# Queries and keys of an attention layer, stored in the order of the products and fetched 128 rows at a time

## The chip, the core and the metric

The kernel runs on one NeuronCore of a Trainium2 chip. A core has five engines that work side by side, each with its own queue, which it works off in order: TensorE (PE) multiplies matrices and writes into PSUM; VectorE (DVE) reduces and combines; ScalarE (ACT) applies functions such as exp; GpSimd (POOL) does the rest; SyncE (SP) issues transfers. Transfers (DMAs) between memory (DRAM) and the core's SBUF are carried out by 16 DMA engines; SP, ACT and POOL can issue them, and an issuing engine that has to wait before it issues holds up everything behind it in its queue.

The metric is the device time of one execution in microseconds (us). Of the kernel before, three runs gave 1357.38, 1358.45 and 1362.58 us; the median is 1358.45 us.

## The reference, cut to what matters

One decoder layer on x of 4 x 1024 tokens x 256 features: self-attention with 16 heads of 16 features, cross-attention to 64 context tokens, and a feed-forward part with ternary weights, each after a layer norm and added to x. The change touches the self-attention only:

```python
qkv = x @ W_qkv + b_qkv                      # x: (B, N, 256), layer-normed
q, k, v = jnp.split(qkv, 3, axis=2)          # each to (B, N, 16 heads, 16)
energy = jnp.einsum('bqhe,bkhe->bqhk', q, k)
attn = jax.nn.softmax(energy, axis=-1) / sqrt(E)
out = jnp.einsum('bihv,bvhd->bihd', attn, v)
x = x + out.reshape(B, N, E) @ W_out + b_out
```

## The kernel before

**Split numbers.** A query or key is kept as two parts: a rounded high part (float32r) and the low rest. One product over 64 rows gives all four cross terms of a head: its rows hold the query as high, high, low, low (16 rows each) and the key as high, low, high, low. A tile `q` or `k` (128 rows x 1024 tokens) holds two heads, 64 rows each: a pair.

**Stages of the self-attention.** The work is cut in 16 units: batch b (4) times group g of four heads (4), and a unit has two pairs. Before a unit come

- `ln1(b)` (L334): layer norm of the batch's x. Statistics on DVE (`bn_stats`, L241), a square root on ACT (L247; its function table has to be loaded, and exp's table again afterwards), normalising (on ACT, L258, after the start-up), transposing on PE, copying out of PSUM on ACT (L279).
- `project(b, c)` (L351): queries and keys of eight heads. For each side (q, k) and each half of the tokens (512), PE makes the product, ACT writes the high part into a tile `hl` (L369), DVE the low part (L370), and one DMA of 512 KB stores `hl` in DRAM (L375) in a tensor of the form part (2) x feature (128) x token (1024). In the very first project, three of the four stores are issued from ACT, and their `hl` come from another set of buffers. Else `hl` has two buffers, and a buffer is free again when its store is done.
- `fetch(u)` (L378): fills the two pairs of `q` and `k` of unit u from those tensors. Each 16 rows of a tile are one DMA of 16 rows x 1024 tokens (64 KB, L393): 32 DMAs for a unit, all on SP. For unit 0 the tokens are taken in halves, so there are 64 DMAs of 32 KB, 16 of them issued from ACT. Buffers of `q` and `k` are four each, so fetch(u + 1) waits until the scores of unit u - 1 are done.

**The order of the work.** PE's, SP's and the pool's DMA order is the program's own order (`ordered`, L54). At the start: `ln1(0)`, `project(0, 0)`, three pieces of it woven into `ln1(0)`; `fetch(0)`; four pieces of `project(0, 1)` (L873); then 16 calls of `top()` (L883), of which every second is followed by a piece of `values(0)`. `top()` is one step of `maxima(u)` (L423): two products of 128 queries with 512 keys and the maximum over the keys on DVE (L446, tile `mx`). The maxima of half a unit are joined (`nm`, L455), rounded (`nm_s`, L458 and L459), transposed on PE and copied out by ACT as `mT` (L464). Then `fetch(1)` is issued, then x of batch 1 (`load_x(1)`, L890), then small weights.

The main loop (L914) has 16 steps for each unit. A step makes the scores of a key block, both pairs (products `q,k` and `mT,sel`, then exp on ACT, L911, tile `exp`), two steps of maxima for the half unit that comes next, and the product of older `exp` tiles with the values. Between them `fill()` puts pieces of `ln1` and `project` of later batches and of the post-processing of earlier ones, by credits that grow towards a due step. `fetch(u + 1)` is called in steps 0 and 1 of unit u; the maxima that need its tiles begin at step 8. After the 16 units the feed-forward part remains.

The order of DVE's and ACT's instructions is not written out: a scheduler places them when the program is built, by the times that it expects, transfers included. Each transfer issued from SP or ACT counts on one of eight semaphores, which are used in turn; a transfer that reuses one waits until the transfer before it on that semaphore has landed. So at most eight are under way.

Of the kernel before, what the change touches and what calls it, by code (L numbers as in the profile page):

```python
# [9 lines left out]
F32 = mybir.dt.float32  # L10
# [7 lines left out]
B, S, E = 4, 1024, 256  # L18
H, D = 16, 16
SK = 64  # L20
HID = 1024
P = 128
# [8 lines left out]
def decoder_layer(ctx, tc, a, out):  # L31
# [15 lines left out]
    nc = tc.nc  # L47
# [14 lines left out]
    def dma(**kwargs):  # L62
        ordered(nc.sync.dma_start(**kwargs))
# [38 lines left out]
    for name in ("wq", "wk"):  # L102
# [5 lines left out]
        t = const.tile([P, E // P, H, D], F32, name=name)  # L108
# [4 lines left out]
    for name in ("bq", "bk"):  # L113

        t = const.tile([P, 2], F32, name=f"{name}_c")
        for g in range(NG):
            r = 64 * (g % 2)
            dma(
                out=t[r : r + 64, g // 2 : g // 2 + 1],
                in_=a[name].rearrange("(j e) g -> g j e", e=32)[g, :, 1 : 1 + D],  # L120
# [35 lines left out]
    dram = main_stack.enter_context(tc.tile_pool(name="dram", bufs=1, space=DRAM))  # L156
# [4 lines left out]
    for i in range(3):  # L161
        t = (const if i else main).tile([P, NT, VW], F32, tag=f"v_sb{i}", name=f"v_sb{i}")
# [28 lines left out]
    def bank():  # L191
        return ps[state["banks"]]()
# [4 lines left out]
    def product(out, terms, start=True, stop=True):  # L197

        n = len(terms)
        strips = [slice(32 * j, 32 * j + 32) for j in range(4)] if state["split"] else [slice(0, P)]  # L200
        for i, (lhsT, rhs) in enumerate(terms):
            for r in strips:
                matmul(
                    out[r, :], lhsT=lhsT[:, r], rhs=rhs, start=start and i == 0,
                    stop=stop and i == n - 1,
                )
# [125 lines left out]
    xnT_of, qk_of, split_of, m_of, pieces_of = {}, {}, {}, {}, {}  # L332

    def ln1(b):  # L334
        mv = main.tile([P, NT, 2], F32, tag="mv1", name="mv1", bufs=2)
        rs = main.tile([P, NT], F32, tag="rs1", name="rs1", bufs=2)
        xnT_of[b] = xnT = main.tile([P, 2, S], F32, tag="xnT", name="xnT")
        n = NT if state["split"] else NT // 2
        for i0 in range(0, NT, n):
            for i in range(i0, i0 + n, 2):  # L340
                yield "free"
                ln_stats(main, mv, [(i + k, b * NT + i + k) for k in range(2)])
            yield "free"
            ln_rstd(main, rs[:, i0 : i0 + n], mv[:, i0 : i0 + n, :])
            for i in range(i0, i0 + n, 4):
                yield "free"
                xn = ln_normalised(post_pool, mv, rs, i, b * NT + i, 4)
                yield "rows"
                ln_transposed(xnT[:, :, i * P : (i + 4) * P], xn)

    def project(b, c):  # L351

        split_of[b, c] = [
            dram.tile([2, P, S], F32, tag=f"kept_{name}", name=f"kept_{name}", bufs=6) for name in "qk"
        ]
        first = (b, c) == (0, 0)

        for side, half in ((0, 0), (1, 0), (1, 1), (0, 1)):
            w, bias = (wq, wk)[side], bqk[("bq", "bk")[side]][:, c : c + 1]
            hl = main.tile([P, 2, 512], F32, tag="exp" if first and half else "hl", name="hl", bufs=4 if first and half else 2)  # L360
            width = 256 if state["split"] else 512
            for i0 in range(0, 512, width):
                yield "cols+"
                cols, part = slice(half * 512 + i0, half * 512 + i0 + width), slice(i0, i0 + width)
                pq = bank()[:, 0:width]
                product(
                    pq, [(w[:, i, c * P : (c + 1) * P], xnT_of[b][:, i, cols]) for i in range(2)]
                )
                nc.scalar.activation(hl[:, 0, part].bitcast(F32R), pq, AF.Identity, bias=bias)  # L369
                nc.vector.scalar_tensor_tensor(  # L370
                    hl[:, 1, part], pq, bias, hl[:, 0, part], ALU.add, ALU.subtract
                )
            cols = slice(half * 512, (half + 1) * 512)
            issue = nc.scalar.dma_start if first and (side or half) else dma
            issue(out=split_of[b, c][side][:, :, cols].rearrange("l p t -> p l t"), in_=hl)  # L375
            pieces_of[b, c] = pieces_of.get((b, c), 0) + 1

    def fetch(u):  # L378

        b, g = divmod(u, NG)  # L380
        pairs = qk_of[u] = []
        rest = []
        for pair in range(2):
            q = main.tile([P, S], F32R, tag="q", name="q", bufs=4)
            k = main.tile([P, S], F32R, tag="k", name="k", bufs=4)
            pairs.append((q, k))
            kept_q, kept_k = split_of[b, g // 2]
            f0 = 64 * (g % 2) + 32 * pair

            def parts(t, kept, order, n, cols, issue, f0=f0):  # L390
                for i, part in enumerate(order):
                    r, f = 64 * n + 16 * i, f0 + 16 * n
                    issue(out=t[r : r + 16, cols].bitcast(F32), in_=kept[part, f : f + 16, cols])  # L393

            if u:
                halves = (slice(0, S),)
            else:
                halves = (slice(0, 512), slice(512, S))
            for n in range(2):
                parts(q, kept_q, (0, 0, 1, 1), n, halves[0], dma)  # L400
            for cols in halves:
                for n in range(2):
                    parts(k, kept_k, (0, 1, 0, 1), n, cols, dma if u or n else nc.scalar.dma_start)
            for n in range(2):
                for cols in halves[1:]:
                    rest.append((parts, q, kept_q, (0, 0, 1, 1), n, cols, dma))
            if pair:
                for f, *args in rest:
                    f(*args)
            yield  # L410

    def values(b):
# [422 lines left out]


    first, parts = ln1(0), project(0, 0)
    for _ in range(10):
        next(first)
# [3 lines left out]
    run(parts)  # L843
    state.update(split=True, pinned=False)
    run(fetch(0))

    sel_f = post_pool.tile([P, 2, P], F32, tag="xn", name="sel_f", bufs=2)
    nc.gpsimd.memset(sel_f, 0.0)
    sel = main.tile([P, 2, P], F32R, name="sel")
    for pair in range(2):  # L850

        for n in range(2):
            c = 64 * n + 2 * pair
# [17 lines left out]


    parts = project(0, 1)  # L873
    for _ in range(5):
        next(parts)
# [11 lines left out]
    run(turning.popleft())  # L887
    due.credit = 0.0
    run(fetch(1))
    load_x(1)  # L890
    loading = late_loads()
# [22 lines left out]
    for u in range(NU):  # L914
        b, g = divmod(u, NG)
# [4 lines left out]
        if g == 0:  # L920
            if b == 0:
                later.add(context(), 6)
                later.add(value_bias(), 1)

            for n in ((1, 2), (), (3,), ())[b]:
                if n > 2:
                    load_x(n)
                due.add(ln1(n), 2)
                due.add(project(n, 0), 8)
                due.add(values(n), 8)  # L930
                if n == 1:
                    due.add(project(n, 1), 8)
            if b % 2:

                due.add(project(b // 2 + 2, 1), 8)
            if b == B - 1:
                load_x(0, view=x_kept, slot=1)
# [4 lines left out]
        for step in range(2 * NT):  # L942
# [3 lines left out]
            if step < 2 and 0 < u < NU - 1:  # L946
                if step == 0:
                    while pieces_of.get(divmod((u + 1) // 2, NG // 2)) != 4:
                        due.step()
                    fetching = fetch(u + 1)  # L950
                next(fetching)
# [151 lines left out]
    halves = 2 * B  # L1103
# [3 lines left out]
    tag = later.tag  # L1107
    while tag is not None or narrows:
        turn += 1
        if tag is not None and turn % 5 in (0, 2):  # L1110
            exps += "Exp" in tag
            tag = next(last, None)
            continue
        sources = []
        if wides:
            i = halves - len(wides)
# [72 lines left out]
```

## Time and profile before

| | before |
|---|---|
| median of three runs | 1358.45 us |
| the profiled execution: its time, its span | 1359.89 us, 1358.1 us |
| PE busy | 1282.7 us (94%), mean granted clock 0.978 |
| DVE busy | 1005.3 us (74%) |
| ACT busy | 896.6 us (66%) |
| DMA queue of SP | 68.47 MB, 16.7% of the 16 engines' time |
| DMA queue of ACT | 2.10 MB, 0.5% |
| stores of `hl` (32 of 512 KB) and fetches (480 of 64 KB, 64 of 32 KB) | 16 MB and 32 MB |

How to read the views of the profile: a line of a group gives the source line, engine, operation, output<-input, the number of instructions, then busy time and mean duration, then how long the engine stood idle just before them and what ended most of it. A line of the time line or of the chain of waits begins with the start and the duration in us. A line of the windows gives a stretch of time, its length, the busy time of PE, PE's weight loads, DVE, ACT and POOL with the number of instructions begun, then PE's granted clock (1.00 is full), the busy share of the 16 DMA engines and the GB/s that they moved.

### The profile page before, as it was taken

Reading aid. Unit: us, or ns where it says so; the run is one execution under the profiler, and the core shown is the slowest. Engines: PE = TensorE matmul, PEld = TensorE weight load, DVE = VectorE, ACT = ScalarE, POOL = GpSimd, SP = SyncE. Lnnn points to the kernel's source line nnn. Section 1 sums busy time; section 2 is a strip of 40 time slices with the busy share of each in tenths; the row PEclk is TensorE's granted clock in tenths of the full one; section 3 lists DMA queues with packets and bytes.
Section 4 is the critical chain, followed back from the end, with each engine's and each line's share of the span. In section 5 each row is a group of like instructions: output and inputs, shape, how many; then the busy total and the mean of one; then the engine's idle time right before and its main releaser. Section 6 shows DMA issues by size and latency. Waiting matters only on the chain.

```text
span 1358.1 us, 27680 instructions
## 1 busy us (share of the span) xinstructions
PE 1282.7 (94%) x11000; PEld 719.2 (53%) x11000; DVE 1005.3 (74%) x2110; ACT 896.6 (66%) x1654; POOL 79.6 (6%) x86
## 2 busy tenths in 40 slices
PE   5889999999999999989999999999999988999987
PEld 2345445545554554444545545545455466776777
DVE  4788877767878877778877767878889357565665
ACT  1277676766677667777676676686766747474765
POOL 4000000022010000011000000010000012000000
PEclk9689999999999999999999999999999989999989
DMA  5431321302020201221111102212210010100000
GB/s 171 133 120 48 109 62 65 95 32 79 33 79 1 63 27 38 71 56 43 53 46 50 45 19 83 75 61 65 63 33 1 2 63 0 51 12 32 1 32 31
DMA packets 46576, 72.72 MB, mean 54 GB/s; under 512 B 11536, under 2 KB 28176, under 8 KB 46448
## 3 DMA queue, kind: packets, MB, share of 16 engines
q1 hardware_dynamic: 44976, 68.47, 16.7%
q10 hardware_dynamic: 1328, 2.10, 0.5%
q8 instruction: 87, 1.43, 0.4%
q0 software_dynamic: 144, 0.39, 0.2%
q14 instruction: 41, 0.34, 0.1%
HBM read 46.81 MB, written 24.12 MB: 52 GB/s over the span
## 4 chain that ended last, share of the span: by engine, by line
PE 75%; DVE 15%; ACT 7%; DMA 2%; issue 1%; SPq 0%; DVEq 0%; ACTq 0%
PE ps_ring L57 44%; PE ps_acc L57 15%; PE ps_wide L57 8%; DVE mx L446 7%; PE ps_misc L57 3%; PE ps_misc L60 2%; ACT exp L911 2%; PE ps_ring L60 2%; DVE nm L605 2%; ACT xn L258 1%; DMA x<-in_x 1%; DVE bn L241 1%; DVE xn L265 1%; DMA q<-kept_q 1%; ACT ex L638 1%
## 5 line engine op out<-in xcount | busy, mean ns | idle before, releaser
L446 DVE TENSOR_REDUCE mx<-ps_ring 128x1 f32<-128x512 f32 x1024 | 646.7, 681 | 154.7 <-PE ps_ring L57 153.7
L911 ACT ACTIVATE exp<-ps_ring 128x512 f32<-128x512 f32 x1024 | 549.3, 607 | 182.6 <-PE ps_ring L57 179.1
L57 PE MATMUL ps_ring<-q,k 64*128 64x512 f32 x1024 | 280.4, 474 | 8.3 <-ACT exp L911 5.9
L57 PE MATMUL ps_ring<-k,q 64*128 64x512 f32 x1024 | 265.3, 428 | 15.6 <-DMA k<-kept_k 4.7
L57 PE MATMUL ps_acc<-exp,v_sb 128*32 128x512 f32 x2048 | 274.5, 608 | 0.0
L57 PE MATMUL ps_ring<-mT,sel 64*128 64x512 f32 x1024 | 233.1, 401 | 0.2 <-ACT mT L464 0.2
L57 PEld LDWEIGHTS ps_ring<-q,k 64*128 64x128 f32 x1024 | 115.9, 185 | 199.0 <-ACT exp L911 68.2
L57 PEld LDWEIGHTS ps_ring<-k,q 64*128 64x128 f32 x1024 | 126.1, 187 | 98.5 <-ACT exp L911 40.9
L57 PEld LDWEIGHTS ps_ring<-mT,sel 64*128 64x128 f32 x1024 | 108.4, 187 | 6.2 <-ACT mT L464 0.7
L57 PEld LDWEIGHTS ps_acc<-exp,v_sb 128*32 128x32 f32 x2048 | 40.5, 108 | 67.2 <-issue 65.4
L1029 DVE BATCH_NORM_STATS2 bnh<-h 128x6 f32<-128x512 f32 x64 | 41.1, 679 | 34.1 <-ACT h L1026 34.0
L1026 ACT ACTIVATE h<-ps_wide 128x1024 f32<-128x1024 f32 x32 | 32.7, 1025 | 42.0 <-PE ps_wide L57 41.9
L1061 DVE SCALAR_TENSOR_TENSOR hl<-ps_misc,lnw,hT 128x512 fp32r<-128x512 f32 x64 | 46.4, 733 | 18.2 <-ACT hT L1060 18.2
L57 PE MATMUL ps_wide<-wfc,xl 128*128 128x512 f32 x128 | 56.6, 443 | 1.9 <-DVE xl L281 1.8
L57 PE MATMUL ps_wide<-wproj,hl 128*128 128x256 f32 x256 | 46.2, 303 | 12.5 <-DVE hl L1061 12.4
L57 PE MATMUL ps_wide<-wfc,xh 128*128 128x512 f32 x128 | 54.2, 423 | 0.0
L1060 ACT ACTIVATE hT<-ps_misc,lnw 128x512 fp32r<-128x512 f32 x64 | 42.6, 686 | 16.3 <-PE ps_misc L60 16.3
L241 DVE BATCH_NORM_STATS2 bn<-x 128x6 f32<-128x256 f32 x96 | 38.9, 416 | 6.6 <-DMA x<-in_x 5.0
L57 PEld LDWEIGHTS ps_wide<-wproj,hl 128*128 128x128 f32 x256 | 34.9, 192 | 16.2 <-DVE hl L1061 14.7
L290 POOL TENSOR_TENSOR x<-x,xbo 128x512 f32<-128x512 f32 x16 | 20.5, 1288 | 367.3 <-ACT xn L258 358.2
L57 PE MATMUL ps_wide<-wproj,hT 128*128 128x256 f32 x256 | 41.4, 285 | 0.0
L60 PE MATMUL ps_misc<-ident,h 128*128 128x128 f32 x256 | 37.4, 274 | 1.0 <-ACT ex L638 0.7
(166 smaller groups left out, 1436.8 us busy)
## 6 DMA issues: line engine op xcount, KB each, us to landing
q<-kept_q SPq DMA_DIRECT2D x240, 64.0 KB
k<-kept_k SPq DMA_DIRECT2D x240, 64.0 KB
kept_q<-hl SPq DMA_DIRECT2D x15, 512.0 KB
kept_k<-hl SPq DMA_DIRECT2D x14, 512.0 KB
out<-x SPq DMA_DIRECT2D x16, 256.0 KB
x<-in_x SPq DMA_DIRECT2D x3, 1024.0 KB
x_kept<-x SPq DMA_DIRECT2D x3, 1024.0 KB
x<-x_kept SPq DMA_DIRECT2D x3, 1024.0 KB
```

Of the source, the lines that this page charges most:

```text
L57: ordered(nc.tensor.matmul(*args, **kwargs))
L60: ordered(nc.tensor.transpose(*args))
L241: pinned(nc.vector.bn_stats(out=st, in_=xs(t)[:, 0, :]))
L258: nc.scalar.activation(xn[:, k, :], xs(t + k)[:, 0, :], AF.Identity, bias=nmr[:, k : k + 1], scale=rs[:, i + k : i + k + 1],)
L290: nc.gpsimd.tensor_tensor(xs(t, 2), xs(t, 2), row.rearrange("p (o d) -> p o d", o=1).to_broadcast([P, 2, E]), ALU.add,)
L446: nc.vector.tensor_reduce(mx[:, t, 2 * pair + n : 2 * pair + n + 1, kh], pm, AX.X, ALU.max)
L605: nc.vector.tensor_reduce(nm[:, t, s, :], pm[s].rearrange("p (h k) -> p h k", k=SK), AX.X, ALU.max, negate=True,)
L911: nc.scalar.activation(ex[:, n, :], pe[n], AF.Exp)
L1026: nc.scalar.activation(h[:, t, :], ph.rearrange("p a f -> p (a f)"), AF.Gelu)
L1029: nc.vector.bn_stats(out=st[:, half, :], in_=h[:, t, half * 512 : (half + 1) * 512])
L1060: nc.scalar.activation(hT, pt, AF.Copy, scale=w)
L1061: nc.vector.scalar_tensor_tensor(hl, pt, w, hT.bitcast(F32), ALU.mult, ALU.subtract)
```

## The change

`project` now stores in the order in which the products take the rows. The tensor has the form head (8) x row block (4) x feature (16) x token; each of the two parts is stored twice, for queries in the blocks 0 and 1 (high) and 2 and 3 (low), for keys in 0 and 2 (high) and 1 and 3 (low). So one store of 512 KB becomes four of 256 KB, and the stored bytes double. `fetch` takes a pair's tile with one DMA: two heads are 128 consecutive rows. Four DMAs of 512 KB for a unit replace 32 of 64 KB; for unit 0, eight DMAs of 256 KB replace 64 of 32 KB, and all of them are now issued from SP. The source of the two forms:

```diff
         split_of[b, c] = [
-            dram.tile([2, P, S], F32, tag=f"kept_{name}", name=f"kept_{name}", bufs=6) for name in "qk"
+            dram.tile([8, 4, D, S], F32, tag=f"kept_{name}", name=f"kept_{name}", bufs=6)
+            for name in "qk"
         ]
...
-            issue(out=split_of[b, c][side][:, :, cols].rearrange("l p t -> p l t"), in_=hl)
+            for i, part in enumerate(((0, 0, 1, 1), (0, 1, 0, 1))[side]):
+                issue(out=split_of[b, c][side][:, i, :, cols], in_=hl[:, part, :])
...
-            kept_q, kept_k = split_of[b, g // 2]
-            f0 = 64 * (g % 2) + 32 * pair
-
-            def parts(t, kept, order, n, cols, issue, f0=f0):
-                for i, part in enumerate(order):
-                    r, f = 64 * n + 16 * i, f0 + 16 * n
-                    issue(out=t[r : r + 16, cols].bitcast(F32), in_=kept[part, f : f + 16, cols])
...
-            for n in range(2):
-                parts(q, kept_q, (0, 0, 1, 1), n, halves[0], dma)
+            h = 4 * (g % 2) + 2 * pair
+            kept_q, kept_k = (
+                t[h : h + 2].rearrange("h i f t -> (h i f) t") for t in split_of[b, g // 2]
+            )
+            halves = (slice(0, 512), slice(512, S)) if u == 0 else (slice(0, S),)
+            dma(out=q[:, halves[0]].bitcast(F32), in_=kept_q[:, halves[0]])
             for cols in halves:
-                for n in range(2):
-                    parts(k, kept_k, (0, 1, 0, 1), n, cols, dma if u or n else nc.scalar.dma_start)
...
+                dma(out=k[:, cols].bitcast(F32), in_=kept_k[:, cols])
+            if u == 0:
+                rest.append((q, kept_q))
             if pair:
-                for f, *args in rest:
-                    f(*args)
+                for q, kept_q in rest:
+                    dma(out=q[:, 512:S].bitcast(F32), in_=kept_q[:, 512:S])
```

In the built program PE's and POOL's orders are the same as before, instruction by instruction. On DVE and ACT the scheduler has placed some instructions elsewhere, which the prediction takes up.

## Prediction

> **What bounds the kernel.** I read the chain that ended last first, then who waits for transfers, then the first 150 us.
>
> ```profile
> PE 75%; DVE 15%; ACT 7%; DMA 2%; issue 1%; SPq 0%; DVEq 0%; ACTq 0%
> ...
> L57 PE MATMUL ps_ring<-k,q 64*128 64x512 f32 x1024 | 265.3, 428 | 15.6 <-DMA k<-kept_k 4.7
> ```
>
> The chain is PE's for three quarters, and DMA has 2% of it. The 1024 products that read `k` and `q` waited for a fetch once, 4.7 us. So where fetches are not at the very start, they are hidden:
>
> ```profile
> 246.51 3.56 SPq L63 DMA_DIRECT2D q<-kept_q  x8
> 250.12 3.67 SPq L63 DMA_DIRECT2D k<-kept_k  x8
> 253.88 3.61 SPq L63 DMA_DIRECT2D q<-kept_q  x8
> 257.54 5.77 SPq L63 DMA_DIRECT2D k<-kept_k  x8
> ```
>
> A unit's 32 issues take 17 us of SP. A unit lasts 64.5 us (62.4 to 1095 us, 16 units), the maxima that need the tiles begin half a unit later, 32 us, and SP waits most of its time for PE and DVE. Taking away 28 of 32 issues saves nothing there. What is left is the start:
>
> ```profile
> 17.06 2.74 DMA kept_q<-hl
> ...
> 20.25 5.43 DMA q<-kept_q
> ...
> 25.70 3.58 DMA q<-kept_q
> ...
> 29.30 1.72 DMA k<-kept_k
> ...
> 42.58 6.81 PE ps_ring L57 x39
> 49.40 10.85 DVE mx L446 x18
> ...
> 60.27 0.20 DVE nm L455
> ```
>
> These are pieces of the chain in order of time. From 17.06 to 31.0 us it is store and fetch; then PE works at a granted clock of 0.50 (the windows have 0.62 in 28 to 31 us, 0.50 until 49 us) after standing idle from 26.3 us; from 49.4 us DVE is the limit, 18 maxima in 10.85 us, 0.60 us each. At 60.5 us the first half's maxima are joined.
>
> **The change part by part.**
>
> *Fetches of unit 0.* 64 issues become 8, 16 of them off ACT, whose queue was held until 35.7 us by them. A gain by itself. From the first product to `nm` took 29.3 us; 32 maxima of 0.61 us and four low parts of 0.43 us on DVE make 21 us if PE's clock stays up. The first product comes at 28 to 35 us, by how long the four stores take. So `nm` would be ready at 50 to 62 us.
>
> *Stores.* Each of 512 KB becomes four of 256 KB. The trace does not show a store whose destination is 8 groups of 16 rows, each group 256 KB from the next. Bounds: the store of before, with the same 2 KB rows, and the transfers of one group of 16 rows. In the windows (columns: stretch, length, busy PE, PE loads, DVE, ACT, POOL, then clock, DMA share, GB/s):
>
> ```profile
> 229.70:230.70 1.00, 1.00 (x11) 0.19 (x10) 1.00 (x6) 1.00 (x2) 0.00 (x0) 1.00 1.00 389
> ...
> 250.00:252.00 2.00, 2.00 (x30) 1.33 (x30) 1.44 (x3) 1.83 (x4) 0.00 (x0) 1.00 0.50 131
> ```
>
> The first is a store: all 16 engines busy, 389 GB/s. The second is fetches of 16 rows: the engines half busy, 131 to 150 GB/s in neighbouring windows. So 256 KB take s = 0.67 us at the one end, 1.8 us (146 GB/s) at the other. I take half of 389 GB/s, s = 1.35 us: nearer to the 16-row form, since the destination is made of such groups, but several stores are queued at once.
>
> The Trainium skill speaks against the change here: "DMA: Bandwidth & Descriptors", section "Why a DMA increments its semaphore by 16 and not by 1", says that a transfer is spread over the largest number of engines, up to 16, that divides the outermost count of both sides. By it the new stores (8 groups) run on 8 engines and the old ones and all fetches on 16; s would be 1.35 us, where spreading over all 16 would leave the 0.67 us of the row above. No row of this case shows a transfer on 8 engines.
>
> *The wait that is added: x of batch 1.* SP issues in order: fetch(0), eight stores of project(0, 1), fetch(1), then `x<-in_x`. Before, x was issued late, at 65.5 us, and its statistics stood far behind in DVE's queue:
>
> ```profile
> 65.53 0.42 SPq L63 DMA_DIRECT2D x<-in_x  x1
> ...
> 85.58 0.74 DVE L241 BATCH_NORM_STATS2 bn<-x 128x6 f32<-128x256 f32 x2
> ```
>
> ```profile
> 63.67 2.06 ACT L911 ACTIVATE exp<-ps_ring 128x512 f32<-128x512 f32 x4
> ...
> 85.05 1.28 ACT L247 ACT_TABLE_LOAD   x1
> ...
> 94.63 2.07 ACT L911 ACTIVATE exp<-ps_ring 128x512 f32<-128x512 f32 x4
> ```
>
> In the changed program's order the first `bn<-x` of batch 1 stands between `nm` (L455) and the rounding `nm_s` (L458). If x has not landed, DVE stands still there; `nm_s`, `mT` on ACT, the scores on PE and all exps are queued behind it, and PE has nothing else.
>
> When does x land? The transfers up to it are 24 stores of 256 KB, 4.2 MB of fetches (12.0 us at 350 GB/s, the rate in the windows from 49 to 52 us), three rows broadcast from POOL (2.7 us: their queue's 0.2% of the span), and x, 3.0 us (1 MB at 345 GB/s, the store of x in the windows from 836 us). The first store begins to move at 17.1 us (its high part is ready at 16.25, 0.85 us from issue to movement). Once, before project(0, 1)'s stores, SP waits for unit 0's last store: 2.0 us for landing, issue and start. x lands at 17.1 + 12.0 + 2.7 + 3.0 + 2.0 + 24 s = 36.8 + 24 s: 52.9, 69.2 or 80 us for s of 0.67, 1.35 or 1.8. DVE goes on at T, the later of `nm` and x: 54.5 (x at 52.9 and some waste in the queues), 69.2 or 80 us.
>
> *The layer norm's place.* Before, exps start 3.4 us after `nm`, and 24 exps on they pause from 85.05 to 94.63 us, for statistics, two tables and seven `xn` in a row; the 28th ends at 96.6. In the changed order the pause comes after four exps and is short, as statistics run while DVE would wait for the scores: two tables (1.28 us each), `sd` 0.30, one `hl` 0.47, 3.4 us in all; `xn` lies between exps. Exps start at T + 3.9 (two `bn` of 0.4 us stand ahead), four take 2.1, the pause 3.4, 24 more 20.8 at the pace of 67.7 to 85.0 us (20 in 17.3 us), and 1.5 for the eight `xn`: T + 31.7. The change is T + 31.7 - 96.6 = T - 64.9: -10.4, +4.3 or +15.1 us.
>
> *x of batch 2.* Its first `bn` stood at 159.2 us and stands in the changed order right behind four maxima that end at 140.6 us in the old time:
>
> ```profile
> 138.16 2.47 DVE L446 TENSOR_REDUCE mx<-ps_ring 128x1 f32<-128x512 f32 x4
> ```
>
> Ahead of that x in SP's queue are the key stores (DVE ready at 129.3 us, moving at 130.2), fetch(2) of 2 MB and x itself: 130.2 + 4 s + 6.0 + 3.0 + 0.6 for landing = 142.5, 145.2 or 147 us. DVE stands 1.9, 4.6 or 6.4 us; PE has about 1 us of banks ahead. +1, +3.6 or +5.4 us. Both times shift alike with what happened before.
>
> *The rest.* The two weight loads `raw` are read some 20 us earlier on DVE, where they land about then: 0 to 1.5 us each; I take 0 and keep the end. Buffers of `hl`: four stores take 5.4 us, the closest stores two apart begin 19 us or more apart (129.3, 146.8, 149.15 us and so on): nothing; without that cover ACT would wait some 5 us each time. `x<-in_x` at 571.6 us is on the chain for 6.3 us before and after, in the same place.
>
> **Sum.** +4.3 + 3.6 = +7.9 us on the profiled 1359.89 us: 1367.8. That execution lies 1.4 us over the median, so against the median it is 1366.4. I give 1367.
>
> **Rivals.**
>
> 1. The stores run at full rate (s = 0.67): -10.4 + 1 = -9.4 us, 1350.5. For it: same bytes a row, same tile, 389 GB/s in the row. Against: the destination's form. It decides from s below about 0.95 us, where the sum turns negative by more than 1 us.
> 2. The stores are as slow as 16-row transfers (s = 1.8): +20.5 us, 1380. For it: 131 GB/s in the row. Against: those transfers are limited by issues of 0.45 us each, as the engines are only half busy.
> 3. The waits are there but cost little, as PE catches up: DVE is busy 74% of the span only, and a stall of `nm_s` also lets later tiles arrive. Then the sum lies at 0 to +6, 1358 to 1365. For it: s of 1.0 to 1.25. Against: PE is busy 94%, so lost time is hardly regained.
>
> **Chances.** Slower stores with both stalls (forecast, with rival 2): 0.52. Rival 3, or s in between: 0.30. Rival 1: 0.18. A difference of 0.5%, 6.8 us, is about what a measurement can tell from no change. Some of the first (0.02) falls within that. So slower by over 0.5%: 0.50, within: 0.32, faster: 0.18. The range 1350 to 1377 takes rival 1's value in and leaves out the last part of rival 2, with 0.1 to 0.2 outside.
>
> **What would show it.** Right: `bn<-x` waits for `x<-in_x` some 10 us at about 58 to 70 us; DMA share near 0.5 while only stores run; no pause of the exps at 85 to 95 us. Wrong: x lands before `nm`; a DMA share of 1.0 at 389 GB/s in the new stores; differences behind 170 us, where I count none.

## The result and the profile after

The changed kernel took 1381.28 us in the median of five runs (1377.94 to 1383.47), the kernel before 1361.89 us in five runs beside them (1357.38 to 1362.58). The ratio is 1.0153, with a 95% interval from 1.0131 to 1.0175: slower by 19.4 us, where 8 were forecast. The time lies 4 us above the range. The profiled execution took 1380.78 us, its span is 1378.6 us, against 1358.1 us of the profiled one before. Line numbers of the changed kernel are some 7 lower behind the change (the maxima are L439, the exps L904).

The page of the changed kernel: the chain's shares, SP's queue, the memory traffic, and the groups of `bn` and of the products of `k` and `q` (busy time and mean, then idle time before them and its cause):

```profile
PE 72%; DVE 14%; ACT 6%; DMA 5%; issue 1%; SPq 1%; ACTq 0%; DVEq 0%
...
q1 hardware_dynamic: 45760, 84.17, 18.3%
...
HBM read 46.81 MB, written 40.89 MB: 64 GB/s over the span
...
L57 PE MATMUL ps_ring<-k,q 64*128 64x512 f32 x1024 | 261.4, 425 | 24.6 <-ACT exp L904 6.4
...
L241 DVE BATCH_NORM_STATS2 bn<-x 128x6 f32<-128x256 f32 x96 | 39.1, 417 | 18.1 <-DMA x<-in_x 16.4
```

DMA has 5% of the chain in place of 2%, and the layer norm's statistics waited 16.4 us for `x`; before, their row had 5.0. SP's queue moves 84.17 MB for 68.47, and 40.89 MB are written for 24.12: the doubled stores are 16.8 MB more. The engines' busy times differ by less than 2 us (PE 1281.8 for 1282.7, DVE 1006.9 for 1005.3, ACT 897.8 for 896.6): nothing computes more slowly, something arrives late.

Where was the time lost? PE makes the same 11,000 products in the same order in both kernels (in e14 and e17 some stand elsewhere between 928 and 1044 us, none of them at a time of the table), so the start of a product in one trace less its start in the other tells how late the kernel is at that place. The table has this offset against the kernel before, in us, at products that began in it at the time on the left. The experiments of the next section stand beside it; each column is one profiled execution.

| product at (before) | after | 128 rows outside (e1) | x early (e5) | own buffer (e7) | read of raw late (e14) | all three (e17) | before with gaps (e9) |
|---|---|---|---|---|---|---|---|
| 31.0, first `k,q` | +9.4 | +2.6 | +8.2 | +7.4 | +7.5 | +9.5 | +3.4 |
| 61.0, `nm_s` turned | +10.8 | -3.1 | +2.6 | +8.9 | +10.5 | +4.1 | +6.4 |
| 95.9 | +7.6 | -7.6 | +3.1 | +5.7 | +6.0 | +5.1 | +6.5 |
| 141.3 | +7.6 | -7.6 | +5.1 | +5.7 | +6.0 | +6.9 | +6.4 |
| 161.9 | +16.3 | -1.9 | +4.9 | +16.3 | +16.7 | +6.7 | +6.4 |
| 178.0 | +14.4 | -3.8 | +3.0 | +14.4 | +14.8 | +4.8 | +6.4 |
| 273.9 | +13.3 | -5.0 | +1.8 | +13.2 | +13.6 | +3.7 | +6.5 |
| 286.9 | +17.2 | -6.8 | +5.8 | +10.9 | +18.6 | +1.4 | +6.5 |
| 567.0 | +17.0 | -7.1 | +5.4 | +10.6 | +18.3 | +1.1 | +10.6 |
| 908.2 | +14.4 | -9.9 | +3.4 | +8.0 | +16.0 | -1.4 | +10.5 |
| 924.0 | +20.4 | -8.9 | +10.8 | +14.6 | +16.0 | -1.4 | +10.5 |
| 1352.9, last | +20.8 | -8.7 | +11.7 | +15.4 | +16.5 | -1.1 | +7.7 |

In the column of the changed kernel the loss falls in four places: 7.6 us up to 96 us, 6.8 us between 141 and 178 (8.7 by 162, of which 1.9 are given back at once), 3.9 us between 274 and 287 (from +11.5 to +17.3 if every product is looked at), 6.0 us between 908 and 924. Besides, 1.1 us are given back between 178 and 274 and 2.8 us between 287 and 908.

**The first place** is the one of the forecast. DVE's time line (start, duration, then idle time just before and what ended it), and the chain of waits ahead of it:

```profile
63.62 0.19 DVE L448 TENSOR_REDUCE nm<-mx 128x16 f32<-128x32 f32 x1
70.75 0.43 DVE L241 BATCH_NORM_STATS2 bn<-x 128x6 f32<-128x256 f32 x1 [6.94 <-DMA x<-in_x]
71.09 0.16 DVE L451 CAST nm_s<-nm 128x16 fp32r<-128x16 f32 x1
```

```profile
53.82 1.47 SPq L63
...
55.33 1.43 SPq L63
...
60.34 10.38 DMA x<-in_x
70.75 0.43 DVE bn L241
```

`nm` is ready at 63.81 us, and DVE stands 6.94 us for `x`, with the rounding `nm_s` queued behind. In the chain, SP's issues of the last two stores take 1.4 us each: SP is held by stores that do not go faster. The windows (stretch, length, busy PE, PE loads, DVE, ACT, POOL, clock, DMA share, GB/s) of two stretches in which only new stores moved:

```profile
26.00:27.00 1.00, 1.00 (x2) 0.34 (x1) 0.00 (x0) 0.00 (x0) 0.00 (x0) 0.50 0.52 201
27.00:28.00 1.00, 1.00 (x2) 0.34 (x1) 0.00 (x0) 0.00 (x0) 0.00 (x0) 0.50 0.52 201
```

Half of the DMA engines, 201 GB/s, though several stores were queued: 256 KB in 1.30 us. The 512 KB store of before had a share of 1.00 and 389 GB/s. That eight engines work all the time, and not sixteen half of it, is in the trace's records of single packets: from 26 to 28 us eight packets are under way at nearly every instant, never fewer than seven, mostly of 2 KB and 84 ns.

**The second place**, x of batch 2, and what PE's clock did there:

```profile
145.75 2.47 DVE L439 TENSOR_REDUCE mx<-ps_ring 128x1 f32<-128x512 f32 x4
153.84 0.43 DVE L241 BATCH_NORM_STATS2 bn<-x 128x6 f32<-128x256 f32 x1 [5.62 <-DMA x<-in_x]
```

```profile
150.00:152.00 2.00, 0.01 (x1) 0.00 (x0) 0.00 (x0) 0.94 (x2) 0.00 (x0) 0.86 0.97 328
152.00:154.00 2.00, 0.00 (x0) 0.00 (x0) 0.16 (x1) 0.00 (x0) 0.00 (x0) 0.50 0.56 206
154.00:156.00 2.00, 1.29 (x5) 0.48 (x9) 2.00 (x5) 0.00 (x0) 0.00 (x0) 0.50 0.10 36
156.00:158.00 2.00, 2.00 (x18) 0.60 (x14) 2.00 (x7) 0.00 (x0) 0.00 (x0) 0.50 0.48 104
```

DVE stands 5.62 us; PE runs dry at 150.0 us and goes on at 154.7 us, 4.7 us, and then works at a clock of 0.50 until some 158.3 us: 21 products that took 2.0 us before take 3.6 us. From 148.8 to 154.7 us the offset grows by 5.2 us, and by 158.3 us by another 1.7 us, to +14.4. The loss of the place is larger than the wait that made it.

The offset then stands at +14.4 until 166.8 us and grows by 1.9 us in the next 6 us; this is no loss. ACT changes function tables there, for the square root of the layer norm of batch 2:

```profile
164.36 1.28 ACT L247 ACT_TABLE_LOAD   x1
...
165.98 1.28 ACT L904 ACT_TABLE_LOAD   x1
```

No exp runs from 164.36 to 167.27 us, and at 167.92 us PE has waited 0.76 us for one. The kernel before changes tables at 165.68 us, which is some 16 us later by its products; there it loses the same, and the offset is back at +14.4 by 178 us. The same step is in e1, whose stores are fast (from -3.7 to -1.9, back to -3.8), and in e5 the layer norm of batch 2 stands earlier and costs 2.0 us there (+3.1 at 96 us, +5.1 at 141 us).

**The third and the fourth place** were not in the forecast. ACT's time line near 297 us, and DVE's near 938 us:

```profile
292.17 0.60 ACT L904 ACTIVATE exp<-ps_ring 128x512 f32<-128x512 f32 x1 [1.69 <-PE ps_ring L57]
296.74 0.47 ACT L371 ACTIVATE hl<-ps_ring,bq_c 128x256 fp32r<-128x256 f32 x1 [3.97 <-DMA kept_k<-hl]
```

```profile
931.09 1.29 DVE L439 TENSOR_REDUCE mx<-ps_ring 128x1 f32<-128x512 f32 x2 [1.13 <-PE ps_ring L57]
938.50 0.69 DVE L744 TENSOR_REDUCE part<-raw 128x1 f32<-128x512 f32 x1 [6.12 <-DMA raw<-in_wfc]
```

ACT wants to write queries into a buffer of `hl` whose four key stores SP issued from 288.22 to 291.57 us. In the kernel before the same instruction waited 0.23 us:

```profile
286.97 0.84 ACT L369 ACTIVATE hl<-ps_ring,bq_c 128x256 fp32r<-128x256 f32 x2 [0.23 <-DMA kept_k<-hl]
```

DVE wants to sum `raw`, whose load was issued at 929.68 us behind a fetch of 2 MB. Before, the first of these sums began at 939.42 us, some 15 us later by the products, and waited for nothing.

### The profile page after: what moved, and what is told of

Its sections match the earlier page's. It is cut to its first block, busy times and chain, and to the rows that moved or that the text cites. A ratio compares the mean times of both kernels' runs of the same rounds, so it can differ in the third digit from the quotient of the medians.

```text
span 1378.6 us, 27288 instructions
## 1 busy us (share of the span) xinstructions
PE 1281.8 (93%) x11000; PEld 715.9 (52%) x11000; DVE 1006.9 (73%) x2110; ACT 897.8 (65%) x1654; POOL 79.7 (6%) x86
## 3 DMA queue, kind: packets, MB, share of 16 engines
q1 hardware_dynamic: 45760, 84.17, 18.3%
HBM read 46.81 MB, written 40.89 MB: 64 GB/s over the span
## 4 chain that ended last, share of the span: by engine, by line
PE 72%; DVE 14%; ACT 6%; DMA 5%; issue 1%; SPq 1%; ACTq 0%; DVEq 0%
PE ps_ring L57 41%; PE ps_acc L57 15%; PE ps_wide L57 8%; DVE mx L439 7%; PE ps_misc L57 3%; PE ps_misc L60 2%; DMA x<-in_x 2%; ACT exp L904 2%; PE ps_ring L60 2%; DVE nm L598 2%; DMA kept_k<-hl 1%; SPq L63 1%; ACT xn L258 1%; DMA raw<-in_wproj 1%; DVE xn L265 1%
## 5 line engine op out<-in xcount | busy, mean ns | idle before, releaser
L439 DVE TENSOR_REDUCE mx<-ps_ring 128x1 f32<-128x512 f32 x1024 | 646.5, 682 | 140.9 <-PE ps_ring L57 139.9
L904 ACT ACTIVATE exp<-ps_ring 128x512 f32<-128x512 f32 x1024 | 549.3, 606 | 182.4 <-PE ps_ring L57 179.1
L57 PE MATMUL ps_ring<-k,q 64*128 64x512 f32 x1024 | 261.4, 425 | 24.6 <-ACT exp L904 6.4
L57 PEld LDWEIGHTS ps_ring<-k,q 64*128 64x128 f32 x1024 | 122.6, 186 | 106.2 <-ACT exp L904 45.3
L1022 DVE BATCH_NORM_STATS2 bnh<-h 128x6 f32<-128x512 f32 x64 | 41.2, 680 | 34.4 <-ACT h L1019 34.3
L57 PE MATMUL ps_wide<-wfc,xl 128*128 128x512 f32 x128 | 56.9, 444 | 1.4 <-DVE xl L281 1.4
L57 PE MATMUL ps_wide<-wproj,hl 128*128 128x256 f32 x256 | 46.0, 302 | 12.6 <-DVE hl L1054 12.5
L1053 ACT ACTIVATE hT<-ps_misc,lnw 128x512 fp32r<-128x512 f32 x64 | 42.6, 687 | 16.3 <-PE ps_misc L60 16.3
L241 DVE BATCH_NORM_STATS2 bn<-x 128x6 f32<-128x256 f32 x96 | 39.1, 417 | 18.1 <-DMA x<-in_x 16.4
L57 PEld LDWEIGHTS ps_wide<-wproj,hl 128*128 128x128 f32 x256 | 34.7, 190 | 16.2 <-DVE hl L1054 14.8
L372 DVE SCALAR_TENSOR_TENSOR hl<-ps_ring,bq_c,hl 128x256 f32<-128x256 f32 (+1 forms) x30 | 14.9, 499 | 37.6 <-ACT hl L371 37.6
L57 PE MATMUL ps_ring<-xnT,wk 128*32 128x256 f32 (+1 forms) x456 | 35.4, 396 | 7.4 <-ACT xnT L279 7.4
```

The lines of the kernel that those rows point to most:

```text
L57: ordered(nc.tensor.matmul(*args, **kwargs))
L241: pinned(nc.vector.bn_stats(out=st, in_=xs(t)[:, 0, :]))
L372: nc.vector.scalar_tensor_tensor(hl[:, 1, part], pq, bias, hl[:, 0, part], ALU.add, ALU.subtract)
L439: nc.vector.tensor_reduce(mx[:, t, 2 * pair + n : 2 * pair + n + 1, kh], pm, AX.X, ALU.max)
L904: nc.scalar.activation(ex[:, n, :], pe[n], AF.Exp)
L1022: nc.vector.bn_stats(out=st[:, half, :], in_=h[:, t, half * 512 : (half + 1) * 512])
```

## The experiments

**Theory**: the destination of a new store is eight groups of 16 rows, and such a store gets half of the DMA engines; each late arrival then stops an engine whose queue holds the way. **Rivals**: the doubled bytes, or the number of stores, or PE's slow start cost the time whatever form the stores have. The ratios are to the kernel before, measured beside each run (medians 1359.75 to 1361.69 us), with their 95% intervals.

### e1: the same bytes and stores, 128 rows on the outside

```diff
-            dram.tile([8, 4, D, S], F32, tag=f"kept_{name}", name=f"kept_{name}", bufs=6)
+            dram.tile([8, D, 4, S], F32, tag=f"kept_{name}", name=f"kept_{name}", bufs=6)
...
+            rows = split_of[b, c][side].rearrange("h f i t -> (h f) i t")
             for i, part in enumerate(((0, 0, 1, 1), (0, 1, 0, 1))[side]):
-                issue(out=split_of[b, c][side][:, i, :, cols], in_=hl[:, part, :])
+                issue(out=rows[:, i, cols], in_=hl[:, part, :])
...
-                t[h : h + 2].rearrange("h i f t -> (h i f) t") for t in split_of[b, g // 2]
+                t[h : h + 2].rearrange("h f i t -> (h f i) t") for t in split_of[b, g // 2]
```

> Kernel after, with the tensor's rows of a head in the order feature, block instead of block, feature, so that the 128 rows that one store writes lie at one even pitch and its destination counts 128 rows instead of 8 groups of 16. Bytes, the number of stores (four of 256 KB), the fetches and the order of every engine stay as in the kernel after. Theory E (a store to 8 groups gets half of the DMA engines): while only stores run the engines' share is about 1.0 at 390 GB/s instead of 0.52 at 200, x of batch 1 lands at about 53 to 56 us instead of 70.7, and the four losses of the kernel after (start 7.5, x of batch 2 7.8, the hl buffer 5.8, the first weight load 4.3 us) shrink to less than half: 1350 to 1362 us. Rival B (the doubled bytes and the four-fold number of transfers cost it): 1375 to 1382 us, as the kernel after.

Measured: 1351.39 us, ratio 0.9933 (0.9917 to 0.995): 30 us faster than the changed kernel, and faster than before. Its windows with only stores, and DVE where `x` was waited for:

```profile
40.00:41.00 1.00, 1.00 (x8) 0.50 (x4) 0.65 (x2) 0.38 (x1) 0.00 (x0) 0.50 1.06 408
41.00:42.00 1.00, 1.00 (x12) 0.30 (x12) 0.85 (x2) 0.00 (x0) 0.00 (x0) 0.50 1.06 399
```

```profile
56.82 0.19 DVE L449 TENSOR_REDUCE nm<-mx 128x16 f32<-128x32 f32 x1
56.92 0.42 DVE L241 BATCH_NORM_STATS2 bn<-x 128x6 f32<-128x256 f32 x1
```

All engines, 400 GB/s (by the packet records mostly sixteen at a time, of 84 ns as well), and `x` is there when `nm` is. Neither the bytes nor the number of stores cost the time; the order of two dimensions of the tensor does.

### e2: as e1, with half as many stores

```diff
-            for i, part in enumerate(((0, 0, 1, 1), (0, 1, 0, 1))[side]):
-                issue(out=rows[:, i, cols], in_=hl[:, part, :])
+            for part in range(2):
+                to = rows[:, part::2, cols] if side else rows[:, 2 * part : 2 * part + 2, cols]
+                issue(out=to, in_=hl[:, part : part + 1, :].to_broadcast([P, 2, 512]))
```

> As e1, but each part goes out in one store of 512 KB whose source is read twice: two stores instead of four. Theory E: as e1, within 4 us, a little faster, since ACT and SP issue half as often in the first 50 us. Rival B: if the number of transfers were the cost, half of the 19 us would come back, 1370 us; if the bytes, none.

Measured: 1353.93 us, ratio 0.9946 (0.9928 to 0.9964). The interval overlaps that of e1: the number of stores, once they run on all engines, shows no effect here.

### e3, e4 and e9: the kernel before with its stores in another form

In e3 and e4 the 512 KB store of before is cut in two of 256 KB, one for each part; e3 writes the rows as eight groups, e4 as 128 rows.

```diff
-            issue(out=split_of[b, c][side][:, :, cols].rearrange("l p t -> p l t"), in_=hl)
+            for part in range(2):
+                rows = split_of[b, c][side][part].rearrange("(h f) t -> h f t", f=16)
+                issue(out=rows[:, :, cols], in_=hl[:, part, :])
```

> Kernel before, with its stores written as two of 256 KB, one a part, and the destination given as 8 groups of 16 rows: the same bytes at the same addresses as e4. Theory E: share of the engines 0.5 at 200 GB/s in a store, 512 KB in 2.7 us; the start-up loses 3 to 8 us against e4. Rival B: 390 GB/s, same time as e4.

> Control of e3: kernel before with two stores of 256 KB, destination given as 128 rows. All theories: 389 GB/s and share 1.0 in a store, and the time of the kernel before within 4 us.

Measured: e3 1361.35 us, ratio 1.0001 (0.9989 to 1.0013); e4 1361.73 us, 1.0006 (0.9996 to 1.0016). The loss expected of e3 did not come, because e3 was not what it was meant to be: groups that lie next to each other in memory are the same as 128 rows, and the built store has 128 rows of 512. It is a second control, and decides nothing. So e9 puts the groups 64 rows apart, as they are in the changed kernel, still with no byte stored twice:

```diff
-            dram.tile([2, P, S], F32, tag=f"kept_{name}", name=f"kept_{name}", bufs=6) for name in "qk"
+            dram.tile([2, 8, 64, S], F32, tag=f"kept_{name}", name=f"kept_{name}", bufs=6)
+            for name in "qk"
...
-            issue(out=split_of[b, c][side][:, :, cols].rearrange("l p t -> p l t"), in_=hl)
+            for part in range(2):
+                issue(out=split_of[b, c][side][part, :, 0:16, cols], in_=hl[:, part, :])
...
-                    issue(out=t[r : r + 16, cols].bitcast(F32), in_=kept[part, f : f + 16, cols])
+                    issue(out=t[r : r + 16, cols].bitcast(F32), in_=kept[part, f // 16, 0:16, cols])
```

> The kernel before, no byte stored twice, each part stored by one transfer of 256 KB into eight groups of 16 rows that lie 64 rows apart, as in the changed kernel; fetches as before, 16 rows each. Theory: the eight groups alone halve the rate: in a stretch with only these stores the DMA share is about 0.5 and the rate about 200 GB/s, and the time rises by 2 to 8 us (1363 to 1369 us), at the start and where hl waits for a buffer near 287 us. Rival: the rate is lost because more stores and twice the bytes are queued; then the share is near 1 and 390 GB/s, and the time is 1359 to 1363 us.

Measured: 1368.57 us, ratio 1.0064 (1.0048 to 1.0079), at the upper end of the expectation; e4, with as many stores of 128 rows, is its control. From 19 to 20 us, after its first four stores and ahead of the first fetch, the DMA share is 0.53 at 178 GB/s, and mostly eight packets are under way. The table shows where: 6.4 us at the start and 4.1 us between 287 and 567 us, for the most part here:

```profile
295.56 0.84 ACT L370 ACTIVATE hl<-ps_ring,bq_c 128x256 fp32r<-128x256 f32 x2 [3.12 <-DMA kept_k<-hl]
```

With the old fetches, the old bytes and half as many stores as the changed kernel has, the eight groups alone cost time. Together e1 and e9 confirm the first half of the theory from both sides.

### e5: x of batches 1 and 2 loaded early

```diff
+    load_x(1)
+    load_x(2)
     parts = project(0, 1)
...
     run(fetch(1))
-    load_x(1)
...
-            if u == 1 and step == 2:
-                load_x(2)
```

> The changed kernel with x of batches 1 and 2 loaded right behind the fetch of unit 0, ahead of the stores of the second projection; the stores keep their form and their rate. Theory: what the slow stores cost is the standing of VectorE for the two loads of x, because these are queued behind the stores. Then the waits of bn for x near 64 and 150 us (6.9 and 5.6 us) go, the exps start about 7 us earlier, the second offset of 7.8 us goes too, and the time is 1366 to 1370 us; what stays is the late first product (40.4 us, nm near 63.8) and the offsets near 292 and 921 us. Rival: it is the traffic itself and the late, slowly clocked start of TensorE that cost the time, wherever x stands in the queue; then the time stays at 1378 to 1384 us and something else waits in place of bn.

Measured: 1369.78 us, ratio 1.0059 (1.004 to 1.0079), 11.5 us less than the changed kernel. `bn` waits 3.2 us in all, and the steps at 61 and at 141 to 162 us are gone from the table. The place of `x` in the queue is the way by which the slow stores reach the path; the late first product (+8.2 us) has become +3.1 us by 96 us.

### e7: a buffer of its own for the bias of the values

`bv_wide`, which POOL writes once, took a turn in the two buffers of `hl`. Queries of the second half then meet the buffer of the stores issued last, not of the ones before.

```diff
-        wide = main.tile([P, 2, P], F32, tag="hl", name="bv_wide", bufs=2)
+        wide = main.tile([P, 2, P], F32, tag="bvw", name="bv_wide")
```

> The changed kernel with the tile that the bias of the values uses (bv_wide) in a buffer of its own, so that it takes no turn in the two buffers of hl. Theory: the offset of 5.8 us near 292 us comes from hl of the queries' second half taking the buffer whose stores were issued some 10 us before; with the turn gone it takes the older one. The wait of ScalarE for kept_k (4.0 us) goes, and the time is 1374 to 1377 us. Rival: the stores are late for either buffer, or the loss is only moved to the next tile; then 1379 to 1383 us.

Measured: 1375.89 us, ratio 1.0111 (1.0096 to 1.0125), 5.4 us less. ACT's `hl` at that place now waits for its product only:

```profile
291.36 0.47 ACT L371 ACTIVATE hl<-ps_ring,bq_c 128x256 fp32r<-128x256 f32 x1 [1.00 <-PE ps_ring L57]
```

### e10, e13 and e14: the read of `raw`

e10 issues the first load of `raw` ahead of the fetch of unit 14.

```diff
-            aside.add(ternary("wfc", 2, HID), 10)
+            wfc = ternary("wfc", 2, HID)
+            next(wfc)
+            next(wfc)
+            aside.add(begun_load(wfc), 10)
...
+    def begun_load(gen):
+        yield "free"
+        yield from gen
```

> The changed kernel with the first load of raw (1 MB, of wfc) issued ahead of the fetch of unit 14 in place of behind it. Theory: the offset of 4.3 us at 921 us comes from VectorE standing 6.1 us for raw, which lies behind 2 MB of fetch and is read earlier in VectorE's order than before; with the load ahead of the fetch the wait goes and the time is 1375 to 1379 us. Rival: the buffer of raw or the fetch is then late in its place, or VectorE's stand only moves; 1380 to 1383 us.

Measured: 1385.03 us, ratio 1.0188 (1.0169 to 1.0206), 3.7 us more. The theory of this run fell. Its DVE:

```profile
931.89 2.46 DVE L744 TENSOR_REDUCE part<-raw 128x1 f32<-128x512 f32 x4 [6.83 <-DMA raw<-in_wfc]
```

The load was issued 7.5 us earlier, at 922.20 us, now right behind four slow stores, and landed 9.7 us after its issue. And the scheduler that writes DVE's order had moved the read forward with it, all four parts at once, so DVE stood longer than in the changed kernel. What matters is the distance between the read and the arrival, not the place of the load. So the next edit leaves the load and moves the read, by a small copy that has to wait for a maximum just made:

```diff
                 for n, pm in enumerate(sides):
...
+                newest[:] = [mx[:, t, 2 * pair + 1, kh : kh + 1]]
                 if at == order[-1]:
...
         part = main.tile([P, len(parts)], F32, tag="part", name="part")
+        if name == "wfc":
+            yield "free"
+            nc.vector.tensor_copy(part, newest[0].to_broadcast([P, len(parts)]))
```

In e13 a second edit slipped in: one piece of the first projection instead of three is woven into the first layer norm (`range(3)` became `range(1)`). e14 is without it.

> The changed kernel with the four parts of raw read some eight maxima later on VectorE: a small copy of a just made maximum into the tile part has to come first (0.15 us more work, overwritten at once). The load of raw keeps its place behind the fetch. The run with the load moved ahead of the fetch gave 1385.0 us, since the parts were then placed earlier too and VectorE stood 6.8 us. Theory: what costs is where the scheduler puts the read, by an arrival that it expects too early, and not the place of the load; then the wait for raw and the offset of 4.3 us at 921 us go, and the time is 1375 to 1378 us. Rival: the parts' own work on VectorE or the traffic costs it wherever they stand; 1380 to 1384 us.

> The changed kernel with the four parts of raw read some eight maxima later on VectorE, and nothing else (the run before also wove fewer pieces of the first projection into the first layer norm, by mistake, and its start differed; from 300 to 921 us its products lay 4 us later than in the changed kernel, after it 0.9 us earlier). Theory: the read stands too early, and with it moved the wait and the offset of 4.3 us go: 1375 to 1378 us. Rival: what is won at 921 us is lost again behind it: 1379 to 1383 us.

Measured: e13 1378.42 us, ratio 1.0129 (1.0112 to 1.0146), which by the second edit says little alone. e14 1376.53 us, ratio 1.0106 (1.0093 to 1.0119), 4.8 us less than the changed kernel. DVE no longer waits for this load:

```profile
941.50 0.17 DVE L747 COPY part<-mx 128x4 f32<-128x4 f32 x1
941.58 1.28 DVE L601 TENSOR_REDUCE nm<-ps_ring 128x8 f32<-128x512 f32 x2
942.78 0.68 DVE L750 TENSOR_REDUCE part<-raw 128x1 f32<-128x512 f32 x1
```

The table's step of 6.0 us at 908 to 924 us is 0.0 in its column.

### e16: is it the start, with ACT held by its issues?

```diff
-            issue = nc.scalar.dma_start if first and (side or half) else dma
+            issue = dma
```

> The changed kernel with all stores of the first projection issued by SP, none by ScalarE. Theory: sixteen stores of 1.35 us from 17.1 us on end at 38.7 us whoever issues them, and x of batch 1 is behind all stores, so VectorE goes on at the same T of about 70 us: 1379 to 1383 us, though ScalarE's second copy of xnT comes earlier than 24.8 us. Rival: ScalarE held for 6.9 us by its issues sets the first product (40.4 us) and the whole start: 1375 to 1378 us.

Measured: 1379.02 us, ratio 1.0128 (1.0115 to 1.0141), at the lower edge of the theory's values, not among the rival's; the interval overlaps that of the changed kernel. But the value came another way than the theory's. ACT's second copy of `xnT` comes early, PE's projection is done sooner, and then the first product waits 17.7 us for its fetch behind the stores, until 44.65 us, 4.3 us later than in the changed kernel. So `nm` is late, `x` is there before it, and DVE waits for nothing, at 66.6 us and not at some 70:

```profile
66.56 0.43 DVE L241 BATCH_NORM_STATS2 bn<-x 128x6 f32<-128x256 f32 x1
```

Of the 6.86 us for which the first four stores issued from ACT hold it in the changed kernel little or nothing is won, because the DMA engines behind them are the limit. This run has the clearest view of them: a stretch in which nothing but queued stores moved.

```profile
34.00:36.00 2.00, 0.00 (x0) 0.00 (x0) 0.00 (x0) 0.00 (x0) 0.00 (x0) 0.50 0.52 202
```

### e11 and e17: all edits on the changed kernel

e11 is e5, e7 and e10 in one; e17 is e5, e7 and e14 in one.

> The changed kernel, its stores still in eight groups, with x of batches 1 and 2 early, bv_wide in its own buffer and raw early. Theory: the three places carry the loss one by one (11.5 us by the run with x early, 5.4 us by the run with the own buffer, 4.3 us by the trace for raw), and removing all gives their sum: 1381.3 - 21.2 = 1360 us, 1357 to 1364 us. Rival: the gains overlap, since a stall that is gone lets the next one grow; 1365 to 1372 us.

> The changed kernel, its stores still in eight groups, with x of batches 1 and 2 early, bv_wide in its own buffer and the parts of raw read later. Theory: the three gains add, 11.5 us and 5.4 us by the runs and 4.3 us by the trace: 1381.3 - 21.2 = 1360 us, 1357 to 1363 us. Rival: gains overlap, as another stall grows where one is gone: 1364 to 1370 us.

Measured: e11 1366.32 us, ratio 1.0046 (1.0031 to 1.006): the rival's value, which e10 explains, since its part costs time in place of winning some. e17 1358.45 us, ratio 0.9981 (0.9969 to 0.9993). The gains of e5, e7 and e14 over the changed kernel, 11.5, 5.4 and 4.8 us, make 21.7, and 1381.3 - 21.7 = 1359.6 us. They add up. With the stores as slow as ever, but nothing standing in a queue for them, the changed kernel is level with the one before.

### e8, e12 and e15: the same moves on e1

e8 is e1 with e5's and e7's edits; e12 has e10's too, e15 has e14's.

> The tensor in the order head, feature, block, token (stores with 128 rows on the outside), with both early loads of x and the own buffer of bv_wide. Theory: with stores on all engines the remaining waits of this kind are x of batch 2 (the gain against the kernel before fell from 7.3 to 1.9 us there, partly given back later) and hl near 292 us (2.7 us): 1343 to 1348 us. Rival: with the stores fast these waits hide behind other limits of VectorE, and the time stays at 1349 to 1353 us.

> The tensor in the order head, feature, block, token with the same three moves. Theory: with the stores on all engines raw waits 2.2 us or less, so it adds at most 2 us to the version without the early raw: 1348 to 1352 us. Rival: the moves work better together than in the run before: 1343 to 1347 us.

> The tensor in the order head, feature, block, token with early loads of x, own buffer of bv_wide and the late read of raw. Theory: raw waits 2.2 us in the version without the late read, so up to 2 us are won: 1348 to 1351 us. Rival: the wait is hidden and the moved read costs as much: 1351 to 1354 us.

Measured: e8 1351.06 us, ratio 0.9924 (0.9908 to 0.994): the rival's value, no more than e1, though its profiled execution ended 3.9 us ahead of that of e1. e12 1353.60 us, ratio 0.9959 (0.9943 to 0.9975): the early load of `raw` costs here too. e15 1347.27 us, ratio 0.99 (0.9883 to 0.9917), by its median the fastest kernel of the study: it beats the kernel before by 14 us and the changed one by 34. The last products of the profiled e8 and e15 end within 0.6 us of each other (-12.6 and -12.0 us against before), so whether the late read of `raw` has a part in it, where only 2.2 us were waited, stays open.

## Why the prediction missed

- **Right: the mechanism.** The stores run at half of the engines. s was taken as 1.35 us and measured as 1.30; rival 1 (full rate) and rival 2 (s = 1.8) are refuted by the windows. The rule that the prediction cited from the Trainium skill ("DMA: Bandwidth & Descriptors", "Why a DMA increments its semaphore by 16 and not by 1") agrees with the share of 0.52 to 0.53 where only stores of eight groups moved (the changed kernel, e9, e16), and with 1.06 in e1, where they have 128 rows.
- **Right: x of batch 1.** T was to be 69.2 us and is 70.75. By the prediction's own T - 64.9, that T gives 5.9 us, and the 28th exp does end 5.9 us late, at 102.6; PE's products are 7.6 us late at 96 us. The term was +4.3: 1.5 us of the miss are T, 1.7 us lie between the exps and PE. The same formula holds in e1: T is 56.9 us, it gives -8.0, and the table has -7.6.
- **Missed, but covered by the wait for x: the start.** The first product was to come at 28 to 35 us and came at 40.36, `nm` was to be ready at 50 to 62 us and was at 63.8. The gain from fewer fetch issues did not show, because the fetches stood behind the slow stores: in the chain of waits a store of keys, issued at 22.78 us, takes 10.2 us to land, and the fetch of `k` behind it 7.2 us. As x came later still, T did not depend on it; with x early (e5) `nm` sets the way.
- **Wrong size: x of batch 2.** The term was +3.6 us and is +6.8. x was to land 145.2 - 140.6 = 4.6 us behind the maxima, and DVE stood 5.62 us; "about 1 us of banks ahead" left PE idle for 4.7 us, as it should by that step. The step that failed is that the idle time was taken as the whole loss. The gap itself moved the products by 5.2 us, and PE went on at a clock of 0.50, worth another 1.7 us by 158.3 us. No slow stretch behind a stall was in the sum.
- **Wrong: "Buffers of `hl`: nothing".** The step took the stores two apart as the ones that share a buffer. It missed that `bv_wide` takes a turn among them. The row that would have shown it was in the trace of before: ACT's `hl` for the queries waits there 0.23 us for `kept_k<-hl`, at 287 us. A wait of 0.2 us is not a nothing; here it said that the cover was used up, and that a slower store would be paid for from there. e7: 5.4 us, and e9 shows the same place in the kernel before.
- **Wrong: the two loads of `raw`, "I take 0 and keep the end".** The prediction's bound was 1.5 us each; the one of `wfc` cost 4.8 us (e14). The fetches in four transfers were expected to be harmless where they are hidden; but the read of `raw` now stands some 15 us earlier among the products, and the load lands behind 2 MB of the fetch only at 938 us. That the scheduler expected it sooner is argued from how it places instructions; e14 shows that moving the read alone ends the wait.
- **Not in the sum: what is given back.** 1.1 us between 178 and 274 us, 1.8 us from there to 281 us (within the third place's row of the table) and 2.8 us between 287 and 908 us. Of the last 1.5 lie at 567 to 586 us, where e1 and e17 have a step back too (to -8.7 and 0.0) and e9, with the old fetches, has none; at 274 to 281 us it is the same (e1 from -5.0 to -6.2, e17 from +3.7 to +2.2, e9 none). So the new fetches may be worth some 3 us, where the prediction said that they save nothing. But these columns share the changed order of DVE and ACT as well, and no run parts the two.
- **Rival 3** (PE catches up) does not hold: the offset behind the second stall is +14.4 us at 158 us of the changed kernel and again at 190 us, and what is given back later is small beside the losses.

The sum by the table: 7.6 + 6.8 - 1.1 + 3.9 - 2.8 + 6.0 + 0.4 = 20.8 us on 1359.89. Two stalls were counted, and both came; four came in all, and the two that were missed are worth 5.4 and 4.8 us. The direction was right; these two, put at nothing, and the two stalls, 3.3 and 3.2 us too small, make up the miss, less what is given back. That rival 2 named 1380 us is chance: its s was not seen.

## What to carry to other kernels

Before an array in memory is put into the reader's order, look at the store's outermost dimension: eight groups with gaps cost half of the DMA engines, and exchanging two dimensions (e1) turned a loss of 1.5% into a gain of 0.7% with the same bytes. When a transfer becomes slower, go through every row of the waits that names it or what is queued behind it, the rows of 0.2 us first, for they can mark places without reserve; and through the buffers by their turns, not by their names. An order that a scheduler has written for an expected arrival is best mended at the reader, as moving the load moves the read along with it.

## What the runs showed of the hardware

- Queued stores of eight groups do not fill each other's gaps: with up to eight under way the share stayed at 0.52 to 0.53, 200 to 203 GB/s, from 30 to 38 us of e16, and from 30 to 36 us its packet records show mostly eight packets of 2 KB at a time, 84 ns each, never fewer than seven. In e1 from 40 to 42 us it is mostly sixteen of the same length. The same page and section of the Trainium skill says that such a transfer takes the lowest-numbered engines of the core; that all stores then share the same eight agrees with these rows, though no record here names the engines.
- Issuing such a store takes SP 0.58 us when nothing is ahead of it (the changed kernel, 128 to 245 us) and 1.1 to 1.6 us in a queue (e16); on ACT single ones held the engine for up to 2.94 us at the start. A store of 128 rows takes SP 0.32 to 0.45 us (e1, 120 to 256 us, but for one of 1.04 us).
- PE's granted clock fell to 0.50 after an idle time of 1.4 us (150.0 to some 151.4 us), 3.7 us (from 18.0 us) and 4.5 us (from 34.3 us) in the trace of the changed kernel, worked out from the mean clock of the 2 us windows. It came back some 3.6 us after work began at 154.7 us. The Trainium skill's page "TensorE: Matmul & The Clock Gate" (Part 1, the HAM clock gate) gives the drop after at least one idle window of some 3.4 us, and the window as free-running; the first of the three is shorter than one window, so there the measurement differs from the page.
